# Loading x through SyncE's queue, and one shared last root for slabs 3 and 7 of a two-layer graph kernel

## The chip, the cores and the metric

The kernel runs on one NeuronCore of a Trainium2 chip. The metric is device time in microseconds (us), the median of several executions; lower is better. A profile is one execution recorded by the hardware profiler. Engines are called by the profile's names: PE is TensorE's matmul (PEld its weight loads), DVE is VectorE, ACT is ScalarE, POOL is GpSimd, SP is SyncE.

## The reference

Two graph layers run one after the other on 4096 nodes with 64 features. The adjacency `adj` is a dense 4096x4096 matrix of zeros and ones, about 16 ones in a row.

```python
# layer 0
support = x @ weight
rank = cumsum(adj != 0, axis=1); deg = rank[:, -1:]; k = minimum(deg, 100)
pos = rank - (deg - k)
w = mask * where(pos > 0, 0.5 ** (k - pos), 0.0)
x = layernorm(x + w @ support + bias)
# layer 1
deg = clip(sum(adj, 1) + 1, 1)
h = (adj @ x + x) / deg
out = relu(concat([x, h], 1) @ W + b)
x = layernorm(x + out / maximum(norm(out), 1e-12))
```

Layer 0 gives each neighbour a weight that halves with every later neighbour in its row. Layer 1 averages the neighbours, applies a dense layer, and divides each row by its length. Each layer ends with a residual sum and a layer norm.

## The kernel before

The adjacency is kept transposed in memory as float32 and is read once. It is cut into 8 slabs of 512 output rows (index `g`), and each slab into 8 tiles (index `k`) of 512 columns. One tile is 512 KB in bfloat16 on chip, and its load converts it. The 64 tile loads (`load_next`, L104) are issued by POOL into one queue, eight ahead at the start and then one in each step of the main loop. Thirty-two buffers hold tiles; from the 33rd tile on, a load also waits until PE has used an older tile for the last time. The loads share eight completion semaphores in turn, so a load also waits for the one eight places before it in POOL's queue to have landed. In the kernel before, the eight loads of x are members of that rotation.

All engines work from an order that is written out by hand. The main loop (L537 to L574) has 64 steps, one per tile. A step counts ones per column block of tiles of the next chunk (`count`, L246), spreads the running counts (`spread`, L264 and L266), makes weights for its own tile (`weigh`: matmuls L276 and L285, then ACT at L292 and DVE at L293), and multiplies the features by the weights of the tile before (`gather`, L303). In the gaps PE sums layer 1's neighbours for slabs whose inputs are ready (`second`, L312). Chunks are single tiles for the first two slabs and pairs or fours later, so PE asks for two tiles at a time from the middle of slab 2 on.

The layer-0 ending of a slab is hung on steps of the next slab through a table of hooks. Three of those hooks concern x: `load_x(g)` (L119) at step 8g+3 brings 128 KB of x for slab g; `add_b0(g)` (L236) on POOL at step 8g+7 adds a bias to it; `first_y(g)` (L419) on DVE at step 8(g+1)+1 adds the result to layer 0's product. POOL runs its instructions in order, so everything behind `add_b0`, further tile loads among it, waits while x has not landed. A second copy of x in another row order, `x_quads`, is loaded by SP at the start, and the weights (`wts`, L199) by SP at about 18.6 us, held back by a small DVE memset (L198). After that SP has only the eight stores of the output.

After the main loop a straight list of calls (L752 to L920) finishes layer 1 for all slabs, in units: slab 6, slabs 4 and 5, slabs 0 and 1, slab 2, slab 3, and slab 7 in two halves, 7b and 7a. A unit's last part takes mean and variance (`last_mv`: L385, L387), then 1/sqrt(variance), an offset -mean times that root (`offset`), and the final scaling (`last_o`: four operations of 128x64 per slab, on ACT at L741 or on DVE at L743), then a store by SP (L750). The root comes in two forms. On POOL it is an addition and a power (L374, L376), with the offset at L733 and L734. For slab 7 it is a square root on ACT (L356), four short DVE operations (L362, L363, L365, L366), and a DVE offset (L731). Slab 3 uses the POOL form, and its four final operations run on ACT before slab 7's last two.

Of the kernel before, what the change touches and what calls it, by code (L numbers as in the profile page):

```python
# [9 lines left out]
F32 = mybir.dt.float32  # L10
# [13 lines left out]
P = 128  # L24
R = 512
TB = R // P
# [13 lines left out]
def adj_resnorm_kernel(  # L40
# [23 lines left out]
    nc = tc.nc  # L64
# [11 lines left out]
    small = ctx.enter_context(tc.tile_pool(name="small", bufs=5))  # L76
# [31 lines left out]
    x1 = const.tile([P, NB, D], F32, name="x1")  # L108
# [7 lines left out]
        nc.sync.dma_start(out=xp[:, bs, :], in_=x_quads[:, bs, :])  # L116

    def load_x(g):
        nc.gpsimd.dma_start(out=x1[:, ts(g, TB), :], in_=x[:, ts(g, TB), :])  # L119


    load_xp(NK // 2, NK)
# [228 lines left out]
    ep = {}  # L351

    def root_a(v, eps, name):

        s = small.tile([P, v.shape[1]], F32, tag="s", name=f"s_{name}")
        nc.scalar.activation(s, v, AF.Sqrt, bias=eps)  # L356
        return s

    def root_b(s, v, eps, name):

        q = small.tile([P, v.shape[1]], F32, tag="q", name=f"q_{name}")
        nc.vector.tensor_tensor(q, s, s, ALU.mult)  # L362
        nc.vector.scalar_tensor_tensor(q, q, eps, v, ALU.add, ALU.add)  # L363
        r = small.tile([P, v.shape[1]], F32, tag="r", name=f"r_{name}")
        nc.vector.reciprocal(q, q)  # L365
        nc.vector.scalar_tensor_tensor(r, s, 2.0, q, ALU.mult, ALU.mult)  # L366
        return r

    def root_p(v, eps, name, tag):

        n = v.shape[1]
        r = small.tile([P, n], F32, tag=tag, name=f"{tag}_{name}")
        if eps:
            nc.gpsimd.tensor_scalar(r, v, eps, None, ALU.add)  # L374
            v = r
        nc.gpsimd.tensor_tensor(r, v, power[:, 0:n], ALU.pow)  # L376
        return r

    def moments(y, name, mv=None):
        n = y.shape[1]  # L380
        st = small.tile([P, n, 6], F32, tag="st", name=f"st_{name}")
        if mv is None:
            mv = small.tile([P, n, 2], F32, tag="mv", name=f"mv_{name}")
        for t in range(n):
            nc.vector.bn_stats(st[:, t, :], y[:, t, :])  # L385
        for t in range(n):
            nc.vector.bn_aggr(mv[:, t, :], st[:, t, :])  # L387
        return mv
# [106 lines left out]
    for g in range(NG):  # L495
        at(NK * g + 3, POOL, load_x, g)
        at(NK * g + 7, POOL, add_b0, g)
        at(min(NK * g + 12, NS - 2), POOL, add_self, g)
# [79 lines left out]
    L = NG - 1  # L578
# [55 lines left out]
    def unit(*slabs):  # L634
        name, bs = "_".join(map(str, slabs)), [g * TB + t for g in slabs for t in range(TB)]
        n = len(bs)
        tiles = []
        for i in range(n // TB):
            tiles.append(a16p.tile([P, 4 * TB // n, n, D], F32, tag="a16", name=f"u_{name}_{i}"))
        four = [t[:, i] for t in tiles for i in range(4 * TB // n)]  # L640
        return name, bs, four
# [51 lines left out]
    def last_y(u):  # L693
        name, bs, (z, _, y, _) = u
        rn = ep["rn", name].unsqueeze(2).to_broadcast([P, len(bs), D])
        nc.vector.scalar_tensor_tensor(y, z, 0.0, rn, ALU.max, ALU.mult)
# [3 lines left out]
        engine = nc.gpsimd if len(bs) >= TB else nc.vector  # L700
        engine.tensor_tensor(y, y, x1[:, rows(bs), :], ALU.add)

    mv_7 = small.tile([P, TB, 2], F32, tag="mv_7", name="mv_7")

    def last_mv(u):
        name, bs, (_, _, y, _) = u
        if len(bs) < TB:
            ep["mv1", str(L)] = mv_7
            t = bs[0] - L * TB
            moments(y, f"l1_{name}", mv_7[:, t : t + 2, :])  # L710
        else:
            ep["mv1", name] = moments(y, f"l1_{name}")

    def last_s(u):
        name = u[0]
        ep["s1", name] = root_a(ep["mv1", name][:, :, 1], eps_ln, f"l1_{name}")

    def last_r(u):
        name = u[0]
        v = ep["mv1", name][:, :, 1]  # L720
        if ("s1", name) in ep:
            ep["r1", name] = root_b(ep["s1", name], v, eps_ln, f"l1_{name}")
        else:
            ep["r1", name] = root_p(v, LN_EPS, name, "r1")

    def offset(u):
        name, bs, _ = u
        mv, r = ep["mv1", name], ep["r1", name]
        off = ep["off", name] = small.tile([P, len(bs)], F32, tag="off", name=f"off_{name}")
        if ("s1", name) in ep:  # L730
            nc.vector.scalar_tensor_tensor(off, mv[:, :, 0], -1.0, r, ALU.mult, ALU.mult)  # L731
        else:
            nc.gpsimd.tensor_tensor(off, mv[:, :, 0], r, ALU.mult)  # L733
            nc.gpsimd.tensor_scalar(off, off, -1.0, None, ALU.mult)  # L734

    def last_o(u, t0, t1, engine=nc.scalar):
        name, bs, (_, _, y, o) = u
        mv, r, off = ep["mv1", name], ep["r1", name], ep["off", name]
        for t in range(t0, t1):
            if engine is nc.scalar:  # L740
                engine.activation(o[:, t, :], y[:, t, :], AF.Identity, bias=off[:, t : t + 1], scale=r[:, t : t + 1])  # L741
            else:
                engine.tensor_scalar(  # L743
                    o[:, t, :], y[:, t, :], mv[:, t, 0:1], r[:, t : t + 1], ALU.subtract, ALU.mult
                )

    def store(u):
        name, bs, (_, _, _, o) = u
        for i, b in enumerate(range(0, len(bs), TB)):
            nc.sync.dma_start(out=out[bs[b] // TB], in_=o[:, b : b + TB, :])  # L750
# [46 lines left out]
    last_pz(u01)  # L797
    last_z(u45)
    last_mv(u6)
    last_relu(u45)  # L800
    last_sq(u45)
# [15 lines left out]
    u2 = unit(2)  # L817
    last_pz(u2)
    last_o(u6, 2, 4)
    last_o(u6, 0, 2)  # L820
    last_y(u45)
    last_rn(u01)
# [13 lines left out]
    own(3, 5)  # L836
    last_add(u01)
    last_mv(u45)
    own_half(1, 1)
    own_half(1, 4)  # L840
# [7 lines left out]
    u3 = unit(3)  # L848
    last_pz(u3)
    last_mv(u01)  # L850
    half_hT(1)
    u7 = unit(L)
# [14 lines left out]
    last_r(u01)  # L867
    own_half(0, 0)
    last_o(u45, 4, 6)
    last_ss(u3)  # L870
    own_half(0, 3)
# [27 lines left out]
    last_rn(u7a)  # L899
    offset(u2)  # L900
    last_o(u01, 6, 8)
    last_r(u3)
    last_y(u7a)
    last_add(u7a)
    last_o(u2, 0, 2)
# [1 line left out]
    last_mv(u7b)  # L907
    last_o(u2, 2, 4)
    last_mv(u7a)
    offset(u3)  # L910
    last_s(u7)
    store(u2)
    last_o(u3, 0, 2)
    last_r(u7)
    last_o(u3, 2, 4)
    offset(u7)
    last_o(u7, 2, 4, nc.vector)
    last_o(u7, 0, 2, nc.scalar)
    store(u3)
    store(u7)  # L920


_INS = ["x", "x_quads", "adjT", "weights"]
# [36 lines left out]
```

## Time and profile before

| | us |
|---|---|
| median of three runs | 242.75 (241.31, 242.75, 243.42) |
| the profiled execution's own time | 241.65 |
| its span (first to last instruction) | 239.6 |
| PE busy | 211.1 (88%) |
| DVE busy | 176.7 (74%) |
| ACT busy | 134.8 (56%) |
| POOL busy | 88.3 (37%) |
| tile loads on POOL's DMA queue | 64, 11.9 from issue to landing (median) |
| x loads on POOL's DMA queue | 8, 10.6 from issue to landing (median) |
| stores by SP | 8, 1.7 from issue to landing (median) |

Busy time counts an engine's work and not its waiting. In lists of waits a row tells which engine and line waited for what, with the total, the number of times and the longest single wait. In timelines a row is the start, the duration, the engine and line, the operation, and in square brackets how long the engine had been idle and what ended that. In tables by stage the columns are the stretch, its length, the busy time of each engine with the number of instructions, the clock that PE was granted (1.00 is full speed), the mean busy share of the DMA engines (it can pass 1 where packets overlap) and the rate.

### The profile page before, as it was taken

To read this page: it belongs to the slowest core of one execution; us is meant where nothing else is said; L and a number is where in the kernel's file an instruction comes from. 1 tells how busy PE (TensorE), PEld (TensorE's weight loads), DVE (VectorE), ACT (ScalarE), POOL (GpSimd) and SP (SyncE) were. 2 spreads that over 40 slices of the span, in tenths; PEclk is the share of its full clock that TensorE was granted. 3 is DMA by queue.
4 is the path that set the end of the run, shared out by engine and by line. 5 is a ranking of instruction groups with operands and counts; after the bars stand their busy time and mean duration, and the time that the engine had idled before them with its cause. 6 is when DMAs were issued, how large, how long until landed. Compare 5 with 4: busy or idle time off the path is not lost.

```text
span 239.6 us, 7388 instructions
## 1 busy us (share of the span) xinstructions
PE 211.1 (88%) x3123; PEld 96.0 (40%) x3167; DVE 176.7 (74%) x451; ACT 134.8 (56%) x203; POOL 88.3 (37%) x164
## 2 busy tenths in 40 slices
PE   8689998889699998999999999999999999996900
PEld 3123334334323442443344334433453454765800
DVE  5459886987488689579758975697569765789981
ACT  5068875787368647565655565455644521171692
POOL 8335625712620540312323151315171000277970
PEclk9799999999799999999999999999999999999975
DMA  6999999999999999999899999999970000000031
GB/s 202 211 211 222 217 213 213 211 215 224 214 213 225 213 213 215 223 211 193 154 173 180 175 202 191 183 168 209 195 155 3 3 0 0 3 0 25 0 107 46
DMA packets 11216, 37.33 MB, mean 156 GB/s; under 512 B 1328, under 2 KB 2480, under 8 KB 11184
## 3 DMA queue, kind: packets, MB, share of 16 engines
q0 software_dynamic: 9600, 34.61, 73.7%
q1 hardware_dynamic: 1584, 2.26, 2.8%
q8 instruction: 24, 0.39, 0.6%
q14 instruction: 8, 0.07, 0.1%
HBM read 69.37 MB, written 1.05 MB: 294 GB/s over the span
## 4 chain that ended last, share of the span: by engine, by line
PE 55%; DMA 17%; POOL 9%; DVE 9%; issue 4%; ACT 4%; ACTq 0%; POOLq 0%; DVEq 0%
PE acc L303 14%; PE acc_part L312 13%; DMA a<-in_adjT_dram 10%; PE v L276 7%; DMA x<-in_x_dram 7%; PE cnt L246 4%; PE v L285 4%; ACT w L292 3%; POOL r L376 3%; PE va L312 2%; DVE w L293 2%; PE rep L264 2%; PE pz L412 2%; PE pi L526 1%; PE va L657 1%
## 5 line engine op out<-in xcount | busy, mean ns | idle before, releaser
L292 ACT ACTIVATE w<-v,less 128x1024 int16<-128x1024 f32 x64 | 71.3, 1114 | 54.2 <-PE v L285 40.9
L293 DVE TENSOR_SCALAR w<-v 128x1024 int16<-128x1024 f32 x64 | 78.2, 1223 | 24.1 <-PE v L285 22.7
L303 PE MATMUL acc<-w,xhl 128*128 128x512 bf16 x236 | 65.9, 383 | 2.7 <-issue 1.4
L104 POOL DMA_DIRECT2D a<-in_adjT_dram x64 | 35.9, 563 | 80.0 <-PE acc_part L312 33.0
L312 PE MATMUL acc_part<-a,x1hl 128*128 128x512 bf16 x135 | 37.1, 381 | 1.8 <-issue 1.4
L303 PEld LDWEIGHTS <-xhl 128*128 128x128 f16 x256 | 23.2, 98 | 35.9 <-issue 12.3
L312 PEld LDWEIGHTS <-x1hl 128*128 128x128 f16 x224 | 18.6, 98 | 30.6 <-issue 13.4
L276 PE MATMUL v<-a,tri 32*32 32x512 bf16 x1024 | 29.9, 388 | 0.7 <-ACT w L292 0.6
L266 ACT ACTIVATE near<-rep,most 128x512 bf16<-128x512 f32 x35 | 23.9, 684 | 9.0 <-PE rep L264 9.0
L285 PE MATMUL v<-near,mine 32*32 32x512 bf16 x1024 | 28.5, 379 | 0.0
L246 PE MATMUL cnt<-a,pick 128*32 128x512 bf16 x256 | 21.8, 389 | 4.8 <-DMA a<-in_adjT_dram 4.1
L256 DVE TENSOR_TENSOR cs<-cnt,cs 128x512 bf16<-128x512 f32 x27 | 18.4, 683 | 7.7 <-PE cnt L246 7.7
L276 PEld LDWEIGHTS <-tri 32*32 32x32 bf16 x1024 | 10.0, 88 | 22.7 <-issue 22.0
L264 PE MATMUL rep<-cs,further 128*128 128x512 bf16 x35 | 13.8, 393 | 2.8 <-DVE cs L256 2.8
L376 POOL TENSOR_TENSOR rn<-ss,power 128x4 f32<-128x4 f32 (+1 forms) x5 | 6.3, 1275 | 26.3 <-DVE ss L679 26.2
L236 POOL TENSOR_TENSOR x<-x,wts 128x256 f32<-128x256 f32 x8 | 5.9, 738 | 22.6 <-DMA x<-in_x_dram 22.6
L231 POOL TENSOR_TENSOR a<-a,ident_b 128x128 bf16<-128x128 bf16 x32 | 12.6, 426 | 0.2
L246 PEld LDWEIGHTS <-pick 128*32 128x32 bf16 x256 | 5.0, 93 | 18.5 <-issue 13.6
L285 PEld LDWEIGHTS <-mine 32*32 32x32 bf16 x1024 | 10.0, 88 | 2.0 <-issue 1.8
L741 ACT ACTIVATE u<-u,off,r 128x64 f32<-128x64 f32 x28 | 10.0, 428 | 0.3 <-POOL off L734 0.3
L657 PE MATMUL va<-wts,hT 128*128 128x64 f32 x64 | 8.0, 276 | 2.4 <-DVE hT L625 1.9
L666 ACT ACTIVATE u<-u 128x256 f32<-128x256 f32 (+1 forms) x5 | 2.5, 502 | 12.4 <-DVE u L662 12.4
(135 smaller groups left out, 242.2 us busy)
## 6 DMA issues: line engine op xcount, KB each, us to landing
a<-in_adjT_dram POOLq DMA_DIRECT2D x64, 512.0 KB, 11.9
c<-in_x_quads_dram SPq DMA_DIRECT2D x2, 512.0 KB, 4.5
x<-in_x_dram POOLq DMA_DIRECT2D x8, 128.0 KB, 10.6
out_dram<-u SPq DMA_DIRECT2D x8, 128.0 KB, 1.7
wts<-in_weights_dram SPq DMA_DIRECT2D x1, 160.0 KB, 7.1
```

The lines of the kernel that those rows point to most:

```text
L104: nc.gpsimd.dma_start(out=a, in_=adjT[g, k])
L246: nc.tensor.matmul(cnt[g][quarters[q], :], lhsT=pick[:, PW - 4 * k : PW - 4 * k + Q], rhs=A[g][k][:, q, :], start=first, stop=last,)
L256: nc.vector.tensor_tensor(new, cnt[g], cs[g], ALU.add)
L264: nc.tensor.matmul(pr, lhsT=further, rhs=cs[g], start=True, stop=True)
L266: nc.scalar.activation(near[g], pr, AF.Relu, bias=most, scale=-1.0)
L276: nc.tensor.matmul(v[e // 2][quarters[q], e % 2, :], lhsT=tri[quarters[e], :], rhs=A[g][k][quarters[e], q, :], start=True, stop=False,)
L285: nc.tensor.matmul(v[e // 2][quarters[q], e % 2, :], lhsT=mine[quarters[e], 4 * k + q, :], rhs=nr[quarters[e], :], start=False, stop=True,)
L292: nc.scalar.activation(w[:, 0:2, :], v[0], AF.Relu, bias=less)
L293: nc.vector.tensor_scalar(w[:, 2:4, :], v[1], -STEP * MAX_NEIGH, 0.0, ALU.add, ALU.max)
L303: nc.tensor.matmul(acc0[g], lhsT=xhl[:, b, :], rhs=w[:, q, :].bitcast(BF16), start=(k, q) == (NK - 1, 0), stop=(k, q) == (0, KB - 1),)
L312: nc.tensor.matmul(acc, lhsT=x1hl[:, b, :], rhs=A[g][b // KB][:, b % KB, :], start=first, stop=last)
L376: nc.gpsimd.tensor_tensor(r, v, power[:, 0:n], ALU.pow)
```

## The change

There are two independent parts.

The first moves the loads of x. `load_x(g)` keeps its place in the hand-written order, but POOL now only writes a zero into one column of the piece's destination (128x1). The load itself is issued by SP. As it overwrites that column, SP waits for the memset, and so the piece isn't loaded earlier than the step that POOL has reached. `add_b0` waits for SP's load. The tile loads alone are left in POOL's queue and in the rotation of its eight semaphores. What x holds and its layout in memory are as before.

The second part joins the last roots of slabs 3 and 7. Their means and variances go into one small buffer `mv_37`, 8 values per row. One root of the ACT and DVE form and one offset, on 128x8 instead of 128x4, serve both; slab 3's POOL root and offset are gone. After the shared offset, slab 7's four final operations come first, two on DVE and two on ACT, then its store; then slab 3's, also two on DVE and two on ACT, and its store.

```diff
     def load_x(g):
-        nc.gpsimd.dma_start(out=x1[:, ts(g, TB), :], in_=x[:, ts(g, TB), :])
+        nc.gpsimd.memset(x1[:, g * TB, 0:1], 0.0)
+        nc.sync.dma_start(out=x1[:, ts(g, TB), :], in_=x[:, ts(g, TB), :])
...
-    mv_7 = small.tile([P, TB, 2], F32, tag="mv_7", name="mv_7")
+    mv_37 = small.tile([P, 2 * TB, 2], F32, tag="mv_37", name="mv_37")
+    slot_of = {3: 0, L: TB}
 
     def last_mv(u):
         name, bs, (_, _, y, _) = u
-        if len(bs) < TB:
-            ep["mv1", str(L)] = mv_7
-            t = bs[0] - L * TB
-            moments(y, f"l1_{name}", mv_7[:, t : t + 2, :])
+        if bs[0] // TB in slot_of:
+            ep["mv1", "37"] = mv_37
+            t = slot_of[bs[0] // TB] + bs[0] % TB
+            moments(y, f"l1_{name}", mv_37[:, t : t + len(bs), :])
         else:
             ep["mv1", name] = moments(y, f"l1_{name}")
...
     def last_o(u, t0, t1, engine=nc.scalar):
         name, bs, (_, _, y, o) = u
-        mv, r, off = ep["mv1", name], ep["r1", name], ep["off", name]
+        if bs[0] // TB in slot_of:
+            n0 = slot_of[bs[0] // TB]
+            mv, r, off = [ep[what, "37"][:, n0 : n0 + TB] for what in ("mv1", "r1", "off")]
+        else:
+            mv, r, off = ep["mv1", name], ep["r1", name], ep["off", name]
...
-    last_r(u3)
     last_y(u7a)
...
     last_mv(u7a)
-    offset(u3)
-    last_s(u7)
+    u37 = ("37", u3[1] + u7[1], None)
+    last_s(u37)
     store(u2)
-    last_o(u3, 0, 2)
-    last_r(u7)
-    last_o(u3, 2, 4)
-    offset(u7)
+    last_r(u37)
+    offset(u37)
     last_o(u7, 2, 4, nc.vector)
     last_o(u7, 0, 2, nc.scalar)
+    store(u7)
+    last_o(u3, 2, 4, nc.vector)
+    last_o(u3, 0, 2, nc.scalar)
     store(u3)
-    store(u7)
```

## The prediction

> **What bounds the kernel now.** I read the busy slices and the table by stage first, since the share of busy time over the whole span mixes stages. In the table the columns after the stretch and its length are PE, PEld, DVE, ACT and POOL busy, then PE's clock, the DMA share and the rate in GB/s.
>
> ```profile
> 0.00:20.00 20.00, 15.48 (x149) 5.49 (x152) 11.22 (x38) 9.24 (x13) 10.25 (x22) 0.91 0.95 210
> 40.00:63.00 23.00, 19.59 (x325) 8.51 (x330) 18.17 (x39) 15.65 (x23) 10.54 (x23) 1.00 1.06 216
> 100.00:150.00 50.00, 48.63 (x799) 20.90 (x811) 37.13 (x76) 27.82 (x36) 14.35 (x28) 1.00 0.98 186
> 230.00:239.60 9.60, 0.00 (x0) 0.00 (x0) 3.66 (x25) 4.79 (x15) 2.36 (x7) 0.54 0.20 68
> ```
>
> There are three stages. Up to about 63 us the DMA engines are full (share near 1, 210 to 216 GB/s) and PE has holes: 23.00 - 19.59 = 3.4 us in the second row. From there to about 226 us PE is the bound: 48.63 of 50 us in the third row. After that PE has nothing left, and a chain of short DVE and ACT operations sets the end.
>
> The waits say who pays for x. They are from two lists, the whole kernel's and PE's alone up to 66 us, with total, times and longest.
>
> ```profile
> POOL x L236 <- DMA x<-in_x_dram: 22.6, 4, 7.0
> ...
> PE cnt L246 <- DMA a<-in_adjT_dram: 4.1, 2, 2.3
> ```
>
> POOL stands 22.6 us for x, but PE's only long waits for a DMA are two for tiles, 2.3 us at the start and 1.8 later. PE's waits between 66 and 180 us hold none for a DMA. The second of the two is in the timeline of 55 to 67 us:
>
> ```profile
> 58.33 0.73 POOL L236 TENSOR_TENSOR x<-x,wts 128x256 f32<-128x256 f32 x1 [6.93 <-DMA x<-in_x_dram]
> 59.00 2.17 POOL L104 DMA_DIRECT2D a<-in_adjT_dram  x4
> ...
> 63.23 0.43 PE L246 MATMUL cnt<-a,pick 128*32 128x512 bf16 x4 [1.83 <-DMA a<-in_adjT_dram]
> ```
>
> The tile that PE waits for at 63.23 was not late because POOL stood: its load was issued at 45.97 (the chain of waits has its DMA from 45.97 for 17.21 us) and lay behind seven others. POOL's 6.93 us ended at 58.33, with four tile loads issued after x still in the queue, some 10 us of work. The queue was never empty, as the share of 1.06 also says. So what matters here is how many bytes go ahead of that tile, not when POOL issues.
>
> The end is in the timelines of the last microseconds, of DVE and of ACT:
>
> ```profile
> 232.19 0.30 DVE L387 BATCH_NORM_AGGREGATE mv<-st_l_7a 128x2 f32<-128x6 f32 x2
> 232.86 0.16 DVE L362 TENSOR_TENSOR q_l<-s_l 128x4 f32<-128x4 f32 x1 [0.36 <-ACT s_l L356]
> 233.72 0.16 DVE L731 SCALAR_TENSOR_TENSOR off<-mv,r_l 128x4 f32<-128x4 f32 x1
> 233.80 0.53 DVE L743 TENSOR_SCALAR u<-u,mv,r_l 128x64 f32<-128x64 f32 x2
> ```
>
> ```profile
> 232.53 0.30 ACT L356 ACTIVATE s_l<-mv,eps_ln 128x4 f32<-128x4 f32 x1
> 232.89 1.43 ACT L741 ACTIVATE u<-u,off,r 128x64 f32<-128x64 f32 x4
> 234.23 0.76 ACT L741 ACTIVATE u<-u,off,r_l 128x64 f32<-128x64 f32 x2
> ```
>
> While DVE computes slab 7's root (232.86 to 233.88), ACT writes slab 3's four outputs, which need POOL's root alone. ACT then does slab 7's last two and ends at 234.99; the last store is issued at 235.01.
>
> **What the Trainium skill says.** "DMA: Bandwidth & Descriptors", section "Issuing engines are not separate DMA queues", says that transfers started by different engines run on the same 16 DMA engines and interleave, so another issuer saves only its issuing time. The trace agrees: SP's weights (160 KB) ran at 22 to 25 us between the tile packets, and the rate stayed at 210 to 215 GB/s. The same page, "Queues, rings and completion order", says that each DMA engine goes round robin between the queues it has work for. The weights agree, landing 7.1 us after issue although tiles take 11.9. So x on SP's queue overtakes the tiles queued ahead of it and takes its turn among those in flight. "TensorE: Matmul & The Clock Gate", section "What's actually happening", says that PE's clock is halved after an idle window of 3.4 us that runs freely. Here 1.8 us of idleness were enough, in the window before 63.46:
>
> ```profile
> 61.40:63.20 1.80, 0.00 (x1) 0.00 (x0) 0.27 (x2) 0.00 (x0) 0.31 (x1) 1.00 1.03 207
> 63.50:66.80 3.30, 2.96 (x40) 0.78 (x37) 2.61 (x10) 1.75 (x2) 2.65 (x6) 0.50 1.08 217
> ```
>
> Matmuls in the second stretch take 0.63 us where 0.38 is usual; summed over its groups against the same groups elsewhere that is 1.46 us.
>
> **The change part by part.**
>
> POOL's issuing. Eight issues of 0.55 us (the x row's median) go; eight memsets come, at 0.10 us each (POOL's 128x1 memsets at the start). That frees 3.6 us on POOL, plus up to 22.6 us of waits. It is worth nothing on the path, because the full queue covers it before 63 us, and after that the loads wait for buffers: POOL's loads wait 33.0 us for PE's L312 and 29.4 for its L264. Without that cover a late load would cost PE up to its own wait, 7 us at the longest.
>
> SP's new waits. Eight loads wait on SP for POOL's memsets. Behind them on SP stand only the stores, the first at 214.9 us; the last memset comes near 174 us. Cost nothing. `add_b0` now waits for SP's load. The weights' 7.1 us stand for x's landing under load; between `load_x` and `add_b0` lie four steps of about 2.46 us, 9.8 in all, so it no longer waits. The tile loads keep eight places of the rotation to themselves; nothing drains, so I count this at zero.
>
> Bytes ahead of the tile at 63.23. Before, x pieces 0 and 1 went ahead of it. Laying the queue's packets in order of start, one tile follows the next after 2.47 us, and after 3.17 and 2.93 us where an x lies between: 0.70 + 0.46 = 1.16 us for two. After, the nearest row is the weights: 128 packets of 1280 bytes at 68 ns, eight per DMA engine, 0.54 us. In proportion to 1024 bytes x takes 0.44. Two pieces are 0.88; piece 2, whose memset comes near 58.5 us and whose data, by the weights' 3.4 us to the first packet, come at about 62, may add up to 0.44. So the tile comes between 0.28 us earlier and 0.16 later. I take -0.1. The bound from below is that x costs nothing among the other packets, -1.16; from above, that each of three costs as much as in POOL's queue, +0.6.
>
> The PE-bound middle. From about 120 us on the second tile of each pair is counted 1.44 to 2.4 us after its last packet, and 1.4 is the least seen while PE was waiting for tiles, so the slack is 0 to 1 us. Before, an x lay behind such a tile, ahead of one with over 4 us. After, it can share the time of the tight one: 0.44 us less the slack, for pieces 4 to 7. I take +0.1 for all, with bounds of 0 (the data come 3.4 us after the memset, on the next pair) and 4 x 0.44 = +1.8.
>
> The tail. Slab 3's POOL work (0.23 + 1.04 + 0.20 + 0.24 us) goes, but its offset was ready at 232.85, as ACT finished its square root; it held nothing up. The moments are complete at 232.49 as before, and the square root ends at 232.83. The five DVE operations on 128x8 in place of 128x4 grow by a few ns each, as the POOL and DVE rows of 8 against 4 columns do (0.17 against 0.16 us at L679), so the offset is there at about 233.90. Only then may ACT start. It stands idle from 232.83 to 233.94 where it wrote slab 3 before, and has four operations left: 1.43 us, to 235.37. DVE's four end at about 234.85, before that. ACT's end moves from 234.99 to 235.37, the last store with it: +0.4 us, bounds +0.3 and +0.5. The moved store of slab 7 leaves at 234.7 and is covered by slab 3's.
>
> Sum: -0.1 + 0.1 + 0.4 = +0.4 us on the profiled execution's own 241.65 (span 239.6 and 2.05 around it). That execution lies 1.1 us under the median of the runs shown, 242.75; I add the change to the median: **243.1**.
>
> **The rivals.**
>
> Faster: x costs nothing on SP's queue, so the tile at 63.23 comes 1.16 us earlier, PE's idleness shrinks from 1.83 to 0.67 us, and the half-clock window, 1.46 us, does not come. 242.75 - 1.16 - 1.46 + 0.4 = 240.5. For it speaks that PE's stall of 0.84 us at 39.4 us, which comes from DVE waiting 1.91 us for POOL's addition, will go. Against it: the bytes are the same, and PE meets the next tile's arrival at 40.96 anyway.
>
> Slower: pieces 4 to 7 fall on the tight tiles of the middle. 4 x 0.44 = 1.8, with the tail's 0.4: 242.75 + 2.2 = 244.9. It decides where a piece takes more than the tile's slack, 0.3 us for most. For it speaks that PE has no slack there (48.63 of 50 us); against it, the 3.4 us of delay.
>
> Not as told: SP's piece lands after `add_b0` is reached, so POOL still waits. The full queue hides it again, and the time is the forecast's, 243.1.
>
> **How the numbers follow.** Forecast 0.64, not as told 0.06, faster rival 0.15, slower rival 0.15. The runs of before differ by 2.1 us among themselves, and a half-clock window more or less is worth 1.5, so single cases are about 1 us wide on each side. The range of 240.9 to 245.0 takes in the unknown costs of the forecast (-1.2 to +1.8 round it, thinned by their small chance) and the greater part of the slower rival; about 0.15 lies outside. One per cent, about what a measurement of this kernel can tell from no change, is 2.4 us: below 240.3 lies some half of the faster rival and a little of the forecast, 0.08; above 245.2 some 0.4 of the slower rival and as much of the forecast as makes 0.10; within 0.82.
>
> **What would show it.** POOL's wait for x at L236 gone or under 3 us, with PE's wait for a tile near 63 us still there. The x loads landing in 5 to 8 us. PE's busy time from 66 to 226 us within 0.5 us of before. In the tail, ACT idle for about 1.1 us after the last L356, and the last store about 0.4 us later after the moments of 7a. I am wrong if the wait near 63 us and the half-clock window go, if PE shows waits for tiles after 120 us, or if ACT does not stand still in the tail.

## The result, and the profile after

The changed kernel takes 240.69 us (median of 22 executions, 239.63 to 242.36), the kernel before 241.78 us (22 executions, 240.94 to 243.99). The ratio is 0.995, with a 95% interval of 0.993 to 0.997: 1.1 us faster. The forecast was 243.1 us from a median of 242.75, so 0.4 us slower. Of the 2.4 us between 243.1 and 240.69, 1.0 is that median, which more executions put lower. The rest is the change. The ratio is within 1% of no change, but the sign is wrong, the time lies 0.2 us below the range of 240.9 to 245.0, and a term of over a microsecond was missing.

The profiled execution of the changed kernel took 242.02 us, with a span of 239.9, the longest span of its 22 executions (median 238.9). The two profiles are therefore compared part by part, not by their spans.

The parts of the prediction first. In the lists of waits of the changed kernel (engine, line and what it waited for; total, times, longest), POOL's wait for x has nearly gone, while its waits for tiles and for PE have grown:

```profile
POOL a L104 <- PE acc_part L313: 44.4, 20, 4.6
...
POOL a L104 <- DMA a<-in_adjT_dram: 26.6, 18, 2.2
...
PE cnt L247 <- DMA a<-in_adjT_dram: 6.5, 9, 2.2
...
POOL x L237 <- DMA x<-in_x_dram: 2.2, 1, 2.2
```

22.6 us became 2.2, and PE gained nothing by it: its wait for the tile near 63 us is still there, 1.74 us long, and ends at 63.06 in place of 63.23. PE's waits for tiles are nine in place of two. The seven new ones are short (0.2 to 0.6 us), and the second part alone, with x on POOL's queue, has ten. The stretches of that wait near 63 us and of the half clock after it are as before (columns as in the first table of the prediction):

```profile
61.40:63.00 1.60, 0.00 (x0) 0.00 (x0) 0.19 (x2) 0.00 (x0) 1.47 (x4) 1.00 1.04 217
63.70:67.00 3.30, 3.30 (x69) 0.78 (x37) 2.51 (x10) 1.80 (x2) 0.70 (x2) 0.50 1.08 222
```

The tail does what was forecast. From the timelines of DVE and of ACT in the changed kernel:

```profile
233.81 0.30 DVE L388 BATCH_NORM_AGGREGATE mv<-st_l_7a 128x2 f32<-128x6 f32 x2
234.48 0.17 DVE L363 TENSOR_TENSOR q_l<-s_l 128x8 f32<-128x8 f32 x1 [0.37 <-ACT s_l L357]
235.38 0.17 DVE L733 SCALAR_TENSOR_TENSOR off<-mv,r_l 128x8 f32<-128x8 f32 x1
235.47 0.98 DVE L749 TENSOR_SCALAR u<-u,mv,r_l 128x64 f32<-128x64 f32 x4
```

```profile
234.14 0.30 ACT L357 ACTIVATE s_l<-mv,eps_ln 128x8 f32<-128x8 f32 x1
235.58 1.44 ACT L747 ACTIVATE u<-u,off,r_l 128x64 f32<-128x64 f32 x4 [1.14 <-DVE off L733]
```

ACT stands idle for 1.14 us and ends at 235.58 + 1.44 = 237.02, that is 2.91 us after the moments (the means and variances) of half 7a are complete at 234.11. Before it was 234.99 - 232.49 = 2.50. So the stores leave 0.41 us later, against the 0.4 forecast.

What was missed comes after the last store. Before, the last store was issued at 235.01 and the span ended at 239.6, 4.6 us later. In the changed kernel it was issued at 237.05 and the span ended at 239.9, 2.9 us later. Each engine closes with an instruction that the profile calls DRAIN, and the program ends when all engines have met after it. SP's list of waits shows this meeting: after its stores SP waits at its closing line (L955 before, L960 after) for the other engines. Before:

```profile
SPq L955 <- PEq L955: 2.4, 2, 1.9
SPq L955 <- DMA out_dram<-u: 1.1, 2, 0.6
```

After:

```profile
SPq L960 <- DMA out_dram<-u: 1.1, 2, 0.6
...
SPq L960 <- PEq L960: 0.7, 2, 0.5
```

The wait of 1.9 us has shrunk to 0.5. The releaser is printed as PE's queue because all closing instructions share one pair of semaphores. The closing line itself, asked for its instructions, shows whose drain is long: POOL's, 6.25 us before and 5.61 after, and no other above 1.5 (duration in ns as min/median/max, then first and last start).

```profile
L955 POOLq DRAIN  x3: 46/93/6251, 232.6 to 239.3; - x3
L955 SPq DRAIN  x3: 7/7/7, 237.1 to 239.1; - x3
```

```profile
L960 POOLq DRAIN  x3: 40/102/5609, 232.1 to 239.7; - x3
L960 SPq DRAIN  x3: 7/7/7, 239.1 to 239.4; - x3
```

POOL's last operations, before and in the changed kernel:

```profile
232.61 0.24 POOL L734 TENSOR_SCALAR off<-off 128x4 f32<-128x4 f32 x1
```

```profile
232.18 0.24 POOL L736 TENSOR_SCALAR off<-off 128x4 f32<-128x4 f32 x1
```

The one of before, slab 3's offset, ended at 232.61 + 0.24 = 232.85. POOL's drain began at 232.57 and ended at 238.82, 5.97 us after that operation, while SP had been ready (all stores seen to land) at 237.07. In the changed kernel POOL's last operation is slab 2's offset; the drain ends at 237.74, 5.32 us after it, and SP, ready at 239.12, comes last.

### The profile page after: what moved, and what is told of

It is laid out like the page before. It is cut to its first block, busy times and chain, and to the rows that moved or that the text cites. A ratio compares the mean times of both kernels' runs of the same rounds, so it can differ in the third digit from the quotient of the medians.

```text
span 239.9 us, 7440 instructions
## 1 busy us (share of the span) xinstructions
PE 216.0 (90%) x3167; PEld 95.9 (40%) x3167; DVE 177.5 (74%) x453; ACT 134.2 (56%) x201; POOL 83.4 (35%) x160
## 3 DMA queue, kind: packets, MB, share of 16 engines
q0 software_dynamic: 9216, 33.56, 72.6%
## 4 chain that ended last, share of the span: by engine, by line
PE 53%; DMA 22%; DVE 11%; POOL 6%; ACT 4%; issue 2%; ACTq 0%; POOLq 0%; DVEq 0%
DMA a<-in_adjT_dram 22%; PE acc L304 14%; PE acc_part L313 13%; PE v L277 7%; PE cnt L247 4%; PE v L286 4%; ACT w L293 3%; PE va L313 2%; DVE w L294 2%; POOL r L377 2%; PE pi L527 2%; PE pz L413 2%; PE rep L265 2%; POOL rn L377 2%; PE va L658 1%
## 5 line engine op out<-in xcount | busy, mean ns | idle before, releaser
L304 PE MATMUL acc<-w,xhl 128*128 128x512 bf16 x256 | 70.1, 384 | 0.0
L313 PE MATMUL acc_part<-a,x1hl 128*128 128x512 bf16 x156 | 40.5, 382 | 0.0
L259 DVE CAST cs<-cnt 128x512 bf16<-128x512 f32 x8 | 5.5, 690 | 5.4 <-PE cnt L247 5.4
L209 POOL TENSOR_TENSOR xr<-c,xhl 128x256 f32<-128x256 f32 x8 | 5.3, 664 | 11.7 <-ACT xhl L207 11.6
L747 ACT ACTIVATE u<-u,off,r 128x64 f32<-128x64 f32 x24 | 8.6, 431 | 0.8 <-POOL off L736 0.8
```

Source lines behind the costliest of these rows:

```text
L304: nc.tensor.matmul(acc0[g], lhsT=xhl[:, b, :], rhs=w[:, q, :].bitcast(BF16), start=(k, q) == (NK - 1, 0), stop=(k, q) == (0, KB - 1),)
L313: nc.tensor.matmul(acc, lhsT=x1hl[:, b, :], rhs=A[g][b // KB][:, b % KB, :], start=first, stop=last)
```

## The experiments

Theory A, formed from these lines: before, POOL's closing drain set the end, 1.75 us after SP. The second part of the change takes POOL's last four operations away, 2.0 us of its schedule, and the first shortens the drain, as its length goes by the number of DMAs that POOL issued (72 before, 64 after: 5.97 / 72 = 0.083 us each, and 64 x 0.083 = 5.3). Theory B is the rival: the stores set the end all along, and the gain comes from x on SP's queue in the main loop.

**The second part alone** (the changed kernel with x back on POOL's queue).

```diff
-        nc.gpsimd.memset(x1[:, g * TB, 0:1], 0.0)
-        nc.sync.dma_start(out=x1[:, ts(g, TB), :], in_=x[:, ts(g, TB), :])
+        nc.gpsimd.dma_start(out=x1[:, ts(g, TB), :], in_=x[:, ts(g, TB), :])
```

> The second part alone; x stays in POOL's queue. Theory A (the end of before was POOL's closing drain, which ends 5.97 us after POOL's last operation, 1.74 us after SP is done with the stores; without slab 3's root POOL's last operation comes 2.0 us earlier): the drain is covered, SP sets the end, ACT's later stores give 0.4 back: 1.3 us faster than before, drain still about 6 us long. Theory B (the stores set the end in both, and the gain comes from x on SP's queue): 0.4 us slower than before.

Measured 240.61 us against 241.53 for before, ratio 0.997 (0.9953 to 0.9986): 0.7 us faster, 0.3 to 1.1. B's sign is wrong. A's is right and its 1.3 us lies outside the interval. In the trace the drain ends at 235.73, 5.97 us after POOL's last operation, and SP is ready at 237.63: the drain is covered (over before SP is ready), as A says.

```profile
L959 POOLq DRAIN  x3: 46/93/6249, 229.5 to 238.2; - x3
L959 SPq DRAIN  x3: 7/7/7, 237.6 to 237.9; - x3
```

**The first part alone** (before, with x on SP's queue).

```diff
-        nc.gpsimd.dma_start(out=x1[:, ts(g, TB), :], in_=x[:, ts(g, TB), :])
+        nc.gpsimd.memset(x1[:, g * TB, 0:1], 0.0)
+        nc.sync.dma_start(out=x1[:, ts(g, TB), :], in_=x[:, ts(g, TB), :])
```

> The first part alone; slab 3 keeps its root on POOL. Theory A (with the drain's length going by the number of DMAs that POOL has issued, 72 to 64, so 5.97 to 5.3 us): POOL's drain still sets the end, 0.65 us earlier; before the tail about +0.2: 0.3 to 0.7 us faster. Theory B: the whole gain and without the tail's loss, 1.5 us faster.

Measured 240.76 against 241.53, ratio 0.9981 (0.9967 to 0.9994): 0.46 us faster, 0.1 to 0.8. That is A's number. POOL's drain ends at 237.79, 5.32 us after its last operation, and still comes last; SP is ready at 236.70.

**Slab 3's root left out** (before, with slab 2's root and offset in its place).

```diff
-    last_r(u3)
...
-    offset(u3)
+    ep["r1", u3[0]], ep["off", u3[0]] = ep["r1", u2[0]], ep["off", u2[0]]
```

> Before, with slab 3's root and offset left out (slab 2's are used in their place), so that POOL's four last operations are gone and nothing else; slab 3's output isn't the reference's. Theory A: POOL's drain ends near 236.8, SP's last wait near 237.1 sets the end, 1.7 us faster than before. Theory B: slab 3's root held nothing up, so the time of before within 0.2 us.

Measured 239.97 against 241.53, ratio 0.9942 (0.9922 to 0.9962): 1.4 us faster, 0.9 to 1.9, with A's 1.7 inside. This is the clearest of the pairs: only four POOL operations are gone, 1.71 us of POOL's busy time. A small part of the gain comes through ACT, which had waited a little for their result:

```profile
233.16 0.30 ACT L356 ACTIVATE s_l<-mv,eps_ln 128x4 f32<-128x4 f32 x1
233.36 1.42 ACT L741 ACTIVATE u<-u,off,r 128x64 f32<-128x64 f32 x4
```

ACT starts slab 3's outputs 0.20 us after the start of its square root; before it was 232.89 - 232.53 = 0.36 (lines in the prediction). That is 0.16 us at the most. In SP's waits of this kernel the closing wait is as short as in the changed one:

```profile
SPq L954 <- PEq L954: 0.7, 2, 0.5
```

**One late POOL operation** in the changed kernel, for whose result nobody waits.

```diff
     last_s(u37)
+    late = small.tile([P, TB], F32, tag="late", name="late")
+    nc.gpsimd.tensor_copy(late, mv_37[:, TB : 2 * TB, 0])
```

> The changed kernel with one small copy added on POOL after the last moments, read by nobody. Theory A: POOL's last operation ends about 0.4 us after the moments, its drain 5.3 us later, some 0.6 us after SP is done: 0.6 us slower than the changed kernel, so 0.5 us faster than before. Theory B: an operation that nobody waits for costs nothing: 1.1 us faster than before, as the changed kernel.

Measured 241.17 against 241.53, ratio 0.998 (0.996 to 0.9999). Against the changed kernel's 0.995 it is 0.7 us slower, near A's 0.6, though the two intervals (the changed kernel's goes to 0.997) overlap. The operation takes 0.19 us and is in POOL's timeline at 233.36:

```profile
233.36 0.19 POOL L918 COPY late<-mv 128x4 f32<-128x4 f32 x1 [1.75 <-DVE mv L388]
```

The drain ends 5.32 us after it, at 238.86, and SP was ready at 238.30: POOL is last again.

**More DMAs on POOL**, small and late, read by nobody: 32, and then 48 (shown), because with 32 the end could be read in two ways.

```diff
+    more = const.tile([P, 48, 4], F32, name="more")
+    for i in range(48):
+        nc.gpsimd.dma_start(out=more[:, i, :], in_=x[:, i % 32, 0:4])
     run(NS, DVE)
```

> The changed kernel with 32 small loads of 2 KB added on POOL after the last tile load, into a place that nobody reads. Theory A (the closing drain's length goes by the number of DMAs that POOL issued, 0.083 us each): 96 x 0.083 = 7.97 us after POOL's last operation in place of 5.32; it passes SP's end by about 1.3 us, so 1.3 us slower than the changed kernel. Rival (the drain goes by bytes or packets): about 5.4 us and no change of the time.

With 32: 242.21 against 241.95, ratio 1.0001 (0.9975 to 1.0028). Against the changed kernel that is 1.2 us slower by the ratios, where A said 1.3. The drain ends 7.93 us after POOL's last operation, close to the 7.97 forecast, although the 32 loads add only 0.07 MB to 33.56 and 1024 packets to 9216 in POOL's queue. But in the profiled execution it ends at 238.93, before SP (240.19), so there it was not what cost the time: PE had run at half clock from 221.93 to 228.76, and the moments of 7a came 4.2 us after POOL's last operation, where it is 1.7 us in the changed kernel.

> The changed kernel with 48 small loads of 2 KB added on POOL after the last tile load (112 DMAs in all). Theory A (0.0828 us of closing drain for each DMA that POOL issued): 9.27 us after POOL's last operation near 231 us, so to about 240.2, past SP's end in every execution; the program ends 0.8 us after it, a span near 241.0, and some 2 us slower than the changed kernel, 1 us slower than before. Rival (32 loads more gave a longer drain, but what they cost came from elsewhere): the time as with 32 loads more, no slower than before.

With 48: 243.42 against 241.83, ratio 1.0063 (1.0044 to 1.0083), 1.5 us slower than before and 2.7 slower than the changed kernel by the ratios. The drain ends at 239.85, 9.23 us after the last operation, and SP was ready at 238.47. The moments of 7a are complete at 233.48, earlier than in the changed kernel's profile (234.11), so the issuing of the 48 loads did not delay what comes before. That is 1.4 us of the 2.7; the profiled execution has the shortest span of its nine (240.6, median 241.6), and the section on the hardware comes back to the rest. The closing line shows the drain:

```profile
L963 POOLq DRAIN  x3: 46/102/9522, 230.3 to 240.4; - x3
L963 SPq DRAIN  x3: 7/7/7, 238.5 to 240.1; - x3
```

**x on SP's queue where the drain is covered anyway** (the kernel without slab 3's root, and x by SP as in the first part alone).

> As e3_no_root_3 (before without slab 3's root and offset, so that POOL's drain is covered; slab 3's output isn't the reference's) with x on SP's queue besides. Theory A (x on SP's queue is worth something only through the drain): within 0.4 us of e3_no_root_3, so 1.2 to 2.0 us faster than before. Theory B (x on SP's queue is worth about 1 us of itself): 2.4 us faster than before or more.

Measured 240.00 against 241.95, ratio 0.9916 (0.9887 to 0.9945); without the move of x it was 0.9942 (0.9922 to 0.9962). The difference, 0.6 us, is smaller than the two intervals allow to call a difference. It is above the 0.4 of A and below the 1 of B, and the intervals exclude neither. The drain ends at 236.50, SP is ready at 237.30.

**The same question on another tail**: the changed kernel with slab 3's last four operations split three to one, with x on SP's queue, and then on POOL's.

```diff
-    last_o(u3, 2, 4, nc.vector)
-    last_o(u3, 0, 2, nc.scalar)
+    last_o(u3, 1, 4, nc.vector)
+    last_o(u3, 0, 1, nc.scalar)
```

> The changed kernel with slab 3's last four operations split three on VectorE and one on ScalarE, in place of two and two. Theory A (SP and the stores set the end of the changed kernel, and ScalarE's last operation sets the last store): ScalarE ends one operation, 0.33 us, earlier and VectorE at about the same time: 0.3 us faster than the changed kernel, 1.4 faster than before. Rival (POOL's drain or something else still sets the end): the time of the changed kernel.

> As e5_balance (three of slab 3's last operations on VectorE, one on ScalarE), but with x in POOL's queue as before: 72 DMAs, drain 5.97 us, still covered by SP's end. Theory A (where the drain is covered, moving x is worth little): within 0.5 us of e5_balance, so 1.0 to 2.0 us faster than before. Theory B (moving x gains of itself): 1 us slower than e5_balance.

With x on SP's queue: 240.23 against 241.95, ratio 0.9922 (0.9897 to 0.9947). ACT's last group is now three operations long:

```profile
234.71 1.11 ACT L747 ACTIVATE u<-u,off,r_l 128x64 f32<-128x64 f32 x3 [1.14 <-DVE off L733]
```

That is 1.11 us in place of 1.44, as forecast. But DVE's five operations take 1.20 us and end with ACT's, and SP is ready 4.84 us after the moments of 7a where it was 5.00 in the changed kernel: the tail is 0.16 us shorter in the trace, not 0.3. With x on POOL's queue: 240.83 against 241.83, ratio 0.9941 (0.9917 to 0.9965). The first is the lowest median of the unreduced kernels, 0.7 us under the changed one by the ratios, though the intervals overlap. The pair differs by 0.5 us in favour of SP's queue, again within the intervals; A's "within 0.5" holds, and B's 1 us is not excluded. There is a third such pair: the changed kernel (0.995) and its second part alone (0.997), 0.5 us the same way, again within the intervals. So a gain of some half a microsecond from x on SP's queue itself, apart from the drain, is neither shown nor excluded.

**`add_b0` one step earlier** in the changed kernel. In its profile two DVE operations near POOL's addition to x are long: L363 took 0.97 us at 68.88 where it takes 0.17 elsewhere, with POOL's L237 beside it.

```profile
68.88 0.97 DVE L363 TENSOR_TENSOR q_l<-s_l 128x4 f32<-128x4 f32 x1
...
69.08 0.74 POOL L237 TENSOR_TENSOR x<-x,wts 128x256 f32<-128x256 f32 x1
```

```diff
-        at(NK * g + 7, POOL, add_b0, g)
+        at(NK * g + 6, POOL, add_b0, g)
```

> The changed kernel with add_b0 one step earlier on POOL (8g+6). Theory A (in the changed kernel POOL's addition runs beside VectorE's root near 69 us and beside its multiplication near 151 us, and holds them by 0.8 and 0.6 us): both go, 0.4 to 1.0 us faster than the changed kernel. Rival (these holds are covered by PE's slack, or new ones come, or POOL waits for x again): within 0.3 us of the changed kernel.

Measured 241.04 against 241.95, ratio 0.9958 (0.9932 to 0.9985): no gain on the changed kernel. The rival is right, and two of its three reasons are seen. The long L363 is gone, POOL waits 6.2 us for x again, and two other DVE operations are longer than usual instead (L429 by 0.97 us at 97.4, L475 by 1.15 at 173.7).

**All in one table.** Times in us from the traces, of one execution each. "POOL" is the end of its closing drain, "SP" the moment when SP has seen all stores land. The program's span ends 0.8 to 0.9 us after the later of the two, in every row.

| kernel | DMAs by POOL | POOL's last operation ends | drain ends after it | moments of 7a | POOL | SP | span |
|---|---|---|---|---|---|---|---|
| before | 72 | 232.85 | 5.97 | 232.49 | **238.82** | 237.07 | 239.6 |
| first part alone | 64 | 232.47 | 5.32 | 232.11 | **237.79** | 236.70 | 238.6 |
| second part alone | 72 | 229.76 | 5.97 | 232.63 | 235.73 | **237.63** | 238.4 |
| no root 3 | 72 | 230.26 | 5.97 | 233.12 | 236.23 | **237.54** | 238.4 |
| no root 3, x by SP | 64 | 231.19 | 5.31 | 232.88 | 236.50 | **237.30** | 238.1 |
| changed kernel | 64 | 232.42 | 5.32 | 234.11 | 237.74 | **239.12** | 239.9 |
| one late operation | 64 | 233.54 | 5.32 | 233.29 | **238.86** | 238.30 | 239.6 |
| three to one | 64 | 231.55 | 5.31 | 233.24 | 236.86 | **238.09** | 238.9 |
| three to one, x by POOL | 72 | 230.47 | 5.97 | 233.34 | 236.44 | **238.18** | 239.1 |
| `add_b0` earlier | 64 | 230.53 | 5.31 | 233.39 | 235.84 | **238.39** | 239.3 |
| 32 DMAs more | 96 | 231.00 | 7.93 | 235.19 | 238.93 | **240.19** | 241.0 |
| 48 DMAs more | 112 | 230.62 | 9.23 | 233.48 | **239.85** | 238.47 | 240.6 |

## Why the prediction was wrong, step by step

**The step that failed is the opening sentence on the tail**: slab 3's POOL work "held nothing up". The reasoning looked for who waited for the offset, found ACT ready at the same moment, and stopped there. ACT's wait was 0.16 us at the most, but the program waited for POOL. The chain of waits of before had pointed that way: its last microseconds ran through POOL's L376, L733 and L734 down to POOL's closing line at 232.57. It then goes on to ACT, and I read no further; how long the drain is stands in the list of the closing line alone.

The term that was left out, from the traces: POOL's end at 238.82 against SP's at 237.07, 1.75 us. With the stores' loss of 0.41, the second part should have been worth -1.3 and not +0.4. Leaving out the root alone measured 1.4 us (0.9 to 1.9), and the second part alone 0.7 (0.3 to 1.1). The rest of the 1.3 is 0.6 us by the middle of that interval and 0.2 at the least. The traces suggest where it went. In the six profiles without a half-clock stretch of PE between 221 and 227 us, POOL ends slab 2's offset 1.7 us before the moments of 7a; in the five with one it is 2.9 us (4.2 in the one with two). In such an execution of before POOL would have waited for slab 3's moments (2.28 us before those of 7a in every profile), ended its four operations (1.96 us, as at 230.89 to 232.85) 0.3 us before the moments of 7a, and its drain 5.7 us after them. SP is ready 5.0 us after them in the second part alone, so the second part would be worth 0.7 us there, and 1.3 where no such stretch comes. This is an estimate from the traces: no profile of before has such a stretch, so how much of the rest it explains is open.

**POOL's issuing, counted at zero**, was wrong by the same omission. The eight issues are worth 0.55 us each while they run, hidden as forecast, but also 0.083 us each in the closing drain: 0.65 us, where the drain is last. The first part alone measured 0.46 us (0.1 to 0.8). Where the drain is covered, as in the changed kernel, a shorter drain gains nothing.

**The bytes ahead of the tile near 63 us**: a small effect was forecast (-0.1), and it is small, but its sign is not shown. The tile is there 0.17 us earlier in the profile after; over all profiles it comes at 63.06 to 63.31 with x on SP's queue and at 62.78 to 63.27 with x on POOL's. One reading behind the estimate was off: while SP's weights ran, from 22 to 25 us, the rate was 234 GB/s and not 210 to 215. The estimate itself holds: by the middle of their packets, two tiles came 0.4 and 0.1 us later than usual there, 0.5 in all against the 0.54 taken.

**SP's new waits**: right. x landed after 6.4 us (median; 5.2 to 7.8) against the 7.1 borrowed from the weights, and one wait of 2.2 us for x was left.

**The PE-bound middle**: +0.1 forecast. In the profile after, PE does wait for a tile once after 120 us, 0.62 us at 152.55 (in none of the other seven with x on SP's queue), and DVE's L363 is held 0.8 us. By the same weight load of PE, counted from the start of the program, the changed kernel is 1.7 us later than before at 171 us. Over all profiles, eight kernels with x on SP's queue lie there between 0.28 us earlier and 1.73 later than before, 0.4 later in the mean; the four with x on POOL's lie between 1.03 earlier and 0.00, 0.5 earlier in the mean. So the loop before the tail was slower with SP's loads, by 0.9 us, in these single executions. A part of that goes with the clock: of the eight, the four that lie 0.55 to 1.73 late had half-clock stretches near 9 and 63 us, and the four that lie 0.15 to 0.28 early had none before 221. Like compared with like, SP's loads are 1.0 us later with these stretches (against before alone) and 0.6 without. By 221 us the difference of the means is 0.3: in five of the eight DVE's L679 (L680 there) is no longer held 0.9 us by POOL's addition near 218, as it is in all four of the others. The three timed pairs with the drain covered (0.5 to 0.6 us in favour of SP's queue) point the other way within their intervals. What moving x is worth there has no sure sign.

**ACT and the stores**: right, 0.41 us against 0.4, with ACT idle for 1.14 against 1.1.

The rivals were wrong too. The faster one (the wait near 63 us and the half clock go) did not happen: the wait is 1.56 to 1.74 us in all eight profiles with x on SP's queue, against 1.82 to 1.86 in the four with x on POOL's, and the half clock behind it stands in the profile after. None of the three knew the closing drain.

## What to carry to other kernels

Ask of every engine when it ends, its closing drain included, and not only who waits for its results: this program ends with the last of them. Look at the span left after the last store is issued, and at the closing line of each engine; here a gap longer than a store's landing was POOL's drain. In these kernels POOL, with 64 to 112 DMAs of its own, needed 5.3 to 9.2 us after its last operation. Unless that operation came so long before SP was ready, POOL set the end; each DMA taken from it shortened its drain by 0.08 us.

## What the runs showed of the hardware that was not expected

POOL's closing drain ended 5.97 us after its last operation with 72 DMAs issued by POOL, 5.32 with 64, 7.93 with 96 and 9.23 with 112: 0.082 to 0.083 us for each, whatever their sizes (512 KB, 128 KB or 2 KB) and although the last had landed over 20 us before. It is not the issuing of DMAs as such: SP issued 19 in the changed kernel, and its drains take 7 ns. With 96 DMAs and no half-clock stretch in the tail, POOL's drain would end 7.93 - 1.69 = 6.2 us after the moments of 7a, 1.2 us after SP; with 112 it would be 2.5 us. These estimates from the table are near the 1.2 and 2.7 us measured with 32 and 48 DMAs more.

PE's half-clock stretches of 3.41 us don't stay in one place from one execution to the next; the mean clock of single executions of before runs from 0.958 to 0.981. In the profile of before one followed the idleness of 1.83 us at 61.4; in that of the second part alone it followed the idleness of 1.93 us near 218.6 instead. The same stretch of work there, in the second part alone:

```profile
218.40:221.70 3.30, 1.37 (x13) 1.14 (x11) 3.30 (x26) 0.37 (x1) 2.61 (x3) 1.00 0.00 0
221.80:225.10 3.30, 3.30 (x18) 2.43 (x18) 3.16 (x25) 2.32 (x8) 3.05 (x6) 0.50 0.00 0
```

and before, with the same idleness:

```profile
218.40:221.70 3.30, 1.37 (x13) 0.99 (x11) 3.30 (x19) 0.37 (x1) 2.57 (x4) 1.00 0.01 2
221.80:225.10 3.30, 3.30 (x32) 3.08 (x32) 3.20 (x23) 1.29 (x4) 3.05 (x6) 1.00 0.00 0
```

18 matmuls in place of 32 in the same time. PE's last weight loads, 1.0 us ahead of before at 221 us, were 0.6 us behind at 227. The other four profiles with one such stretch there lose the same against before, 1.66 or 1.67 us. So one in the tail is worth 1.6 to 1.7 us, more than the whole change, and single profiles cannot be compared by their spans.
